# Graph kernel: residual rows of the inverse transforms on half the outputs and last in their sum, and one more turn between edges and message sums

## The chip, the cores and the metric

The kernel runs on one core of one Trainium2 chip. The metric is the device time of the whole program in microseconds (us). Before the change the median of three runs is 2021.49 us (2019.66 to 2024.59). The profiled execution took 2019.38 us, with 2017.7 us from its first to its last instruction and a mean granted TensorE clock of 0.981.

Names of engines below: PE is TensorE, DVE VectorE, ACT ScalarE, POOL GpSimd, SP the engine that queues most loads. PEld is PE's loading of weights.

## The reference, cut to what matters

There are 128 graphs of 128 nodes with 256 channels, all in float32. Layer 0, to which the change belongs, works on the normalised and rectified input `h`:

```
xc     = transpose(x)                                  # x is h here
h      = relu(bn1(conv1d(xc, conv1_w)))                # kernel width 1
h      = bn2(conv1d(h, conv2_w, pad 8))                # kernel width 17 along the nodes
x_conv = relu(h + xc)
s      = x @ w_se.T + b_se                             # three numbers per node
A      = exp(-|s_n - s_m|^2) * mask
msg    = relu(x @ w_msg.T + b_msg)
x_nmp  = A @ msg
x_in   = concat(x_conv, x_nmp)
...                                                    # a GRU cell on x_in and x gives the layer's output
```

Layer 1 is a graph convolution over the first 25 nodes of each graph, in five groups.

## The kernel before

**Front, 0 to about 537 us.** The wide convolution is done by Fourier transforms of length 80 over two windows of 64 outputs each (`OUTW`, `LW`). The spectra of the weights, the normalisation, the narrow convolution, the spectra of the nodes and the products of spectra are made here. For each graph the products are 2 x 80 = 160 rows of 256 channels, in DRAM (`yd`). The change doesn't touch this part, but it makes what the inverse transform reads.

**The loop over 32 blocks of four graphs (`BB = 4`), about 537 to 1880 us.** A block's convolution output, messages and edges are prepared in `beside_gates(i + 1)` while the gates of block i are computed in `gates(i, ...)`. The gates are four units of seven products each (a Strassen scheme, all matmuls of line 552). After each product `between()` is called, which is `step` in the main loop: that makes 28 turns in a block. A turn with an odd number advances `beside_gates` by one `yield`; an even turn, or an odd one once `beside_gates` has ended, advances layer 1, where a part of it is waiting. The fourth unit calls `nxt` at its fifth product; that runs what is left of `beside_gates` and then `gate_inputs(i + 1)`.

In `beside_gates` the steps are, in this order: messages in two halves (line 458), the inverse transform of the first 128 channels (`conv_out`, lines 441 and 443), the transposes of the edges' terms (478), the inverse transform of the other 128 channels, the edges (`edges`: one matmul at 491, an exp on ACT at 493, the product with the mask on DVE at 494), a step of `back` (the end of an earlier block; line 722 on PE and 727 on DVE), and the messages' sums in two halves (`x_nmp`, line 504). `back` also has steps beside the earlier ones. With the turns counted so, the edges come at turn 11 and the two halves of the sums at turns 15 and 17.

**The inverse transform.** The first 128 of a graph's 160 rows lie in the partitions of `ym`, one matrix per graph. The other 32 rows (`NR = 2 * LW - P`) of the four graphs are stacked in the 128 partitions of `yr`. For 128 channels, one matmul with `yr` as weights and the block-diagonal constant `idr` as moving operand fills a PSUM bank of 4 x 128 outputs with the residual rows' share; four matmuls with `ym` and the constant `idm` add the main rows' share, graph by graph:

```
nc.tensor.matmul(ps, yr[:, o * P:(o + 1) * P], idr, start=True, stop=False)
for b in range(BB):
    nc.tensor.matmul(ps[:, b * N:(b + 1) * N], ym[:, b, o * P:(o + 1) * P], idm,
                     start=False, stop=b == BB - 1)
```

DVE then scales and adds (446), and ACT rectifies into `xc` (447). All the residual rows belong to the second window, so their columns of `idr` for the first 64 outputs of each graph hold zeros.

**What sets the order.** PE's instructions follow the program's order; a scheduler lays the instructions of the other engines and the loads in order of readiness, each in a queue of its own. PSUM is a pool of eight banks that go round.

Of the kernel before, what the change touches and what calls it, by code (L numbers as in the profile page):

```python
# [8 lines left out]
F32 = mybir.dt.float32  # L9
# [4 lines left out]
P = 128  # L14
# [3 lines left out]
BB = 4  # L18
HG = 64
OUTW = 64  # L20
LW = 80
NP_ = LW // 2
WCH = 64
NR = 2 * LW - P
# [50 lines left out]
def gnn_kernel(ctx: ExitStack, tc: tile.TileContext, io, out0: bass.AP, out1: bass.AP):  # L75
    nc = tc.nc
    x, adjT = io["x"], io["adjT"]
    B, N, D = x.shape
    C = D // P
    NBLK = B // BB  # L80
    T = BB * N
# [10 lines left out]
    def bank():  # L92
        return psum.tile([P, 512], F32, tag="bank", name="bank")
# [6 lines left out]
    gt = hc.tile([P, LW], F32)  # L100
    vec = cst.tile([P, NV], F32)
    fd = hc.tile([P, 2 * LW], F32)
    idm = cst.tile([P, N], F32)
# [272 lines left out]
    wk = ctx.enter_context(tc.tile_pool(name="wk", bufs=1))  # L376
# [17 lines left out]
        loaded[i] = at, ym, yr  # L394
        hts[i] = ht

    idr = wk.tile([P, T], F32)
    nc.sync.dma_start(idr, io["idr"])

    lr = wk.tile([P, 2, BB, 32], F32)  # L400
# [33 lines left out]
    def conv_out(i):  # L434

        ht = hts[i]
        _, ym, yr = loaded[i]
        xc = wk.tile([P, C, T], F32, tag="xc", name="xc", bufs=2)
        for o in range(C):
            ps = bank()  # L440
            nc.tensor.matmul(ps, yr[:, o * P:(o + 1) * P], idr, start=True, stop=False)  # L441
            for b in range(BB):
                nc.tensor.matmul(ps[:, b * N:(b + 1) * N], ym[:, b, o * P:(o + 1) * P], idm,  # L443
                                 start=False, stop=b == BB - 1)
            u = wk.tile([P, T], F32, tag="el", name="u", bufs=2)
            nc.vector.scalar_tensor_tensor(u, ps, sc2[:, o:o + 1], ht[:, o, :], op0=ALU.mult, op1=ALU.add)
            nc.scalar.activation(xc[:, o, :], u, AF.Relu, bias=sh2[:, o:o + 1])
            yield
        xcs[i] = xc

    def messages(i):

        ht = hts[i]
        msg = wk.tile([P, BB, D], F32, tag="msg", name="msg", bufs=1)
        for b in range(BB):
            ps = bank()
            for c in range(C):
                nc.tensor.matmul(ps[:, :D + 3], ht[:, c, b * N:(b + 1) * N], wms[:, c, :], start=c == 0, stop=c == C - 1)  # L458
            nc.vector.tensor_tensor(msg[:, b, :], ps[:, :D], bms[:, :D], op=ALU.add)  # L459
            nc.vector.tensor_tensor(lr[:, 1, b, 0:3], ps[:, D:D + 3], bms[:, D:], op=ALU.add)  # L460
            if b % 2:
                nc.scalar.activation(msg[:, b - 1:b + 1, :], msg[:, b - 1:b + 1, :], AF.Relu)  # L462
                if b == 1:
                    yield
        msgs[i] = msg
        sv = lr[:, 1, :, 0:3]
        nc.vector.tensor_scalar(lr[:, 0, :, 0:3], sv, 2.0, None, op0=ALU.mult)
        s2 = wk.tile([P, BB, 3], F32, tag="sse", name="sse", bufs=2)
        nc.vector.tensor_mul(s2, sv, sv)
        nc.vector.reduce_sum(lr[:, 1, :, 3:4], s2, axis=AX.X)  # L470
        nc.vector.tensor_scalar(lr[:, 0, :, 4:5], lr[:, 1, :, 3:4], -1.0, None, op0=ALU.mult)
        yield

    def edge_terms(i):

        ps = bank()
        for k in range(2):
            nc.tensor.transpose(ps[:, k * P:(k + 1) * P], lr[:, k].rearrange("p b r -> p (b r)"), ident)
        lt = wk.tile([P, P], F32, tag="lt", name="lt", bufs=2)
        nc.scalar.copy(lt, ps[:, :P])  # L480
        rt = wk.tile([P, BB, N], F32, tag="rt", name="rt", bufs=1)
        nc.vector.tensor_tensor(rt, ps[:, None, P:2 * P].to_broadcast([P, BB, N]),
                                bm[:, :, None].to_broadcast([P, BB, N]), op=ALU.mult)
        lrs[i] = lt, rt

    def edges(i):

        at, _, _ = loaded.pop(i)
        lt, rt = lrs.pop(i)
        pd = bank()  # L490
        nc.tensor.matmul(pd, lt, rt.rearrange("p b n -> p (b n)"), start=True, stop=True)
        e = wk.tile([P, BB, N], F32, tag="e", name="e", bufs=1)
        nc.scalar.activation(e.rearrange("p b n -> p (b n)"), pd, AF.Exp)
        nc.vector.tensor_mul(e, e, at)  # L494
        A_s[i] = e

    def x_nmp(i):

        e, msg = A_s.pop(i), msgs.pop(i)
        xn = wk.tile([P, C, T], F32, tag="xn", name="xn", bufs=2)  # L500
        for c in range(C):
            ps = bank()
            for b in range(BB):
                nc.tensor.matmul(ps[:, b * N:(b + 1) * N], msg[:, b, c * P:(c + 1) * P], e[:, b, :],  # L504
                                 start=True, stop=True)
            if c:
                nc.vector.tensor_copy(xn[:, c, :], ps)
            else:
                nc.scalar.copy(xn[:, c, :], ps)
            yield  # L510
        xns[i] = xn
# [162 lines left out]
    def back_loads(i):  # L674

        ae = l1.tile([P, GW], F32, tag="ae", name="ae", bufs=1)
        nc.sync.dma_start(ae[:n4], io["adjE"][i])
        dc = l1.tile([P, GW], F32, tag="dce", name="dce", bufs=1)
        nc.sync.dma_start(dc, dvf.rearrange("t p -> (t p)")[i * GW:(i + 1) * GW].partition_broadcast(P))
        return ae, dc  # L680
# [207 lines left out]
    def beside_gates(i):  # L888

        ends = back(i - 2, *back_loads(i - 2)) if i > 1 else iter(())  # L890
        if i < NBLK:
            parts = messages(i)
            next(parts)
            yield
            next(parts)
            next(ends, None)
            yield
            inverse = conv_out(i)
            next(inverse)
            next(ends, None)  # L900
            yield
            edge_terms(i)
            next(ends, None)
            yield
            for _ in inverse:
                yield
            edges(i)
            yield
            next(ends, None)
            yield  # L910
            yield from x_nmp(i)
        for _ in ends:
            yield
            if i == NBLK:
                yield
# [4 lines left out]
    for _ in beside_gates(0):  # L920
        pass
# [46 lines left out]
def _spectral_constants():  # L968

    import numpy as np  # L970

    f = np.arange(1, NP_)

    def rows(t):

        t = np.asarray(t)
        c = np.cos(2 * np.pi * np.outer(np.arange(NP_ + 1), t) / LW)
        s = np.sin(2 * np.pi * np.outer(np.arange(NP_ + 1), t) / LW)
        return c, s

    gt = np.zeros((P, NP_, 2))
    fd = np.zeros((P, 2, NP_, 2))
    inv = np.zeros((2, NP_, 2, P))
    c, s = rows(np.arange(KW))
    for r in range(4):
        k = slice(32 * r, 32 * r + KW)
        gt[k, 0, 0], gt[k, 0, 1] = c[0], c[NP_]
        gt[k, 1:, 0], gt[k, 1:, 1] = c[f].T, s[f].T
    for w in range(2):
        n0, n1 = max(0, w * OUTW - PAD), min(P, w * OUTW + OUTW + PAD)  # L990
        c, s = rows(np.arange(n0, n1) - (w * OUTW - PAD))
        fd[n0:n1, w, 0, 0], fd[n0:n1, w, 0, 1] = c[0], c[NP_]
        fd[n0:n1, w, 1:, 0], fd[n0:n1, w, 1:, 1] = c[f].T, (-s[f] - c[f]).T
        c, s = rows(np.arange(OUTW))
        n = slice(w * OUTW, (w + 1) * OUTW)
        inv[w, 0, 0, n], inv[w, 0, 1, n] = c[0] / LW, c[NP_] / LW
        inv[w, 1:, 0, n], inv[w, 1:, 1, n] = 2 * c[f] / LW, -2 * s[f] / LW
    inv = inv.reshape(2 * LW, P)
    idr = np.zeros((BB, NR, BB, P))
    for b in range(BB):  # L1000
        idr[b, :, b] = inv[P:]
    d = {"gt": gt.reshape(P, LW), "fd": fd.reshape(P, 2 * LW), "idm": inv[:P], "idr": idr.reshape(P, BB * P)}
    return {k: np.ascontiguousarray(v, dtype=np.float32) for k, v in d.items()}


def _lay_out(a):
# [18 lines left out]
    d["w2t"][:, :KW] = w2  # L1025
    d["w2t"] = d["w2t"].reshape(P, 2, -1, WCH // 4, P)
    d.update(_spectral_constants())
    d["wms"] = cc(np.concatenate([w["w_msg"], w["w_se"]]).T)
    d["bms"] = cc(np.concatenate([w["b_msg"], w["b_se"]]))
# [60 lines left out]
```

## Time and profile before

| stretch, us | length | PE busy | DVE busy | ACT busy | POOL busy | granted clock |
|---|---|---|---|---|---|---|
| 0 to 537, front | 537 | 495.78 | 311.89 | 158.47 | 152.26 | 0.94 |
| 537 to 1880, loop | 1343 | 1320.56 | 937.62 | 494.40 | 431.22 | 1.00 |
| 1880 to 2018, end | 138 | 132.41 | 65.34 | 52.43 | 17.19 | 1.00 |

Busy times are unions: two overlapping instructions of one engine count once. A float32 matmul of the program is two records in the trace, so counts of PE are twice those in the code. A record's duration holds its latency as well, which overlaps the next record; how fast PE streams is seen from the distance of starts, or in the chain of waits, whose pieces abut. In the loop a block without layer 1 takes 38.9 us, from one matmul on `e` to the next block's.

### The profile page before, as it was taken

The page shows a single profiled execution, that of the slowest core. Times are in us where ns is not written, and L with a number is a line of the kernel's source. Part 1 is how long each engine was busy: PE and PEld are TensorE (multiplying, and loading weights), DVE is VectorE, ACT ScalarE, POOL GpSimd, SP SyncE. Part 2 cuts the span into 40 slices and gives each one's busy share as a digit, 9 for nine tenths or more (in the row PEclk, how much of TensorE's full clock was granted, in tenths as well). Part 3 has the DMA queues.
Part 4 walks back from the last instruction along what each step waited for, and adds up shares of the span by engine and source line. Part 5 has one row for each costly group of instructions (what it writes and reads, how often), then busy time and mean ns, then how long its engine had stood idle before and what let it go on. Part 6 is the DMA issues. An engine that isn't in the chain of part 4 may idle for free.

```text
span 2017.7 us, 29868 instructions
## 1 busy us (share of the span) xinstructions
PE 1948.7 (97%) x10418; PEld 1665.4 (83%) x10418; DVE 1314.8 (65%) x3287; ACT 705.3 (35%) x1406; POOL 600.7 (30%) x681
## 2 busy tenths in 40 slices
PE   8899998999899999999999999999999999999998
PEld 7888877988678888888878888888878888888887
DVE  6667445845477676777755676777755677777643
ACT  3334113421133333333334434333334433333344
POOL 3111441125233343343321143343322143343300
PEclk8899999999899999999999999999999999999999
DMA  9883885459843223223323523223322523321225
GB/s 353 329 284 117 283 280 183 157 170 308 247 134 88 66 74 98 71 68 89 105 68 83 154 69 99 76 69 78 113 71 81 155 70 91 83 69 41 61 81 154
DMA packets 248421, 265.89 MB, mean 132 GB/s; under 512 B 106802, under 2 KB 223751, under 8 KB 243663
## 3 DMA queue, kind: packets, MB, share of 16 engines
q1 hardware_dynamic: 239935, 225.71, 38.2%
q10 hardware_dynamic: 8336, 38.28, 4.9%
q8 instruction: 83, 1.36, 0.3%
q14 instruction: 67, 0.55, 0.1%
HBM read 178.79 MB, written 85.14 MB: 131 GB/s over the span
## 4 chain that ended last, share of the span: by engine, by line
PE 84%; DVE 6%; DMA 5%; issue 2%; POOL 2%; ACT 1%; SPq 0%; DVEq 0%; POOLq 0%; ACTq 0%
PE bank L552 39%; PE bank L307 6%; PE bank L458 6%; PE bank L871 5%; PE bank L223 5%; PE bank L811 5%; PE bank L504 3%; PE bank L238 3%; PE bank L302 3%; PE bank L443 3%; PE bank L441 3%; DMA ln<-in_x_dram 2%; PE bank L790 1%; PE bank L209 1%; DVE e L494 1%
## 5 line engine op out<-in xcount | busy, mean ns | idle before, releaser
L552 PE MATMUL bank<-t,sw 128*128 128x256 f32 x1152 | 291.1, 380 | 0.0
L565 POOL TENSOR_TENSOR u<-u,m 128x256 f32<-128x256 f32 x128 | 92.9, 726 | 654.6 <-ACT m L563 590.2
L552 PEld LDWEIGHTS bank<-t,sw 128*128 128x128 f32 x1152 | 213.4, 190 | 29.6 <-issue 2.8
L552 PE MATMUL bank<-t,wih 128*128 128x256 f32 x768 | 197.3, 379 | 0.0
L552 PEld LDWEIGHTS bank<-t,wih 128*128 128x128 f32 x768 | 143.2, 190 | 18.9 <-issue 0.5
L299 POOL TENSOR_TENSOR vs<-v 128x512 f32<-128x512 f32 x78 | 102.2, 1330 | 139.5 <-DMA v<-vd 53.8
L223 PE MATMUL bank<-wc,ht 128*128 128x256 f32 x512 | 127.2, 404 | 13.1 <-ACT ht L210 11.9
L458 PE MATMUL bank<-wms,ht 128*128 128x259 f32 x512 | 125.3, 388 | 5.2 <-DMA ht<-htd 5.2
L223 PEld LDWEIGHTS bank<-wc,ht 128*128 128x128 f32 x512 | 102.4, 205 | 30.4 <-ACT ht L210 15.0
L458 PEld LDWEIGHTS bank<-wms,ht 128*128 128x128 f32 x512 | 99.3, 194 | 21.0 <-issue 5.6
L552 PE MATMUL bank<-xc,wih 128*128 128x256 f32 x384 | 114.7, 380 | 0.0
L552 PE MATMUL bank<-xn,wih 128*128 128x256 f32 x384 | 114.5, 380 | 0.0
L552 PE MATMUL bank<-t,whh 128*128 128x256 f32 x384 | 114.4, 379 | 0.0
L871 PE MATMUL bank<-w,hh 128*125 128x256 f32 (+9 forms) x480 | 113.5, 380 | 0.5 <-DVE hh L816 0.5
L552 PE MATMUL bank<-ht,whh 128*128 128x256 f32 x384 | 110.4, 381 | 0.0
L297 DVE SCALAR_TENSOR_TENSOR s<-X 128x256 f32<-128x256 f32 x78 | 47.8, 615 | 90.7 <-PE bank L307 90.3
L811 PE MATMUL bank<-ax,w 128*128 128x500 f32 (+8 forms) x416 | 106.9, 396 | 0.0
L462 ACT ACTIVATE msg<-msg 128x512 f32<-128x512 f32 x64 | 40.3, 630 | 173.8 <-DVE msg L459 161.0
L157 POOL TENSOR_TENSOR rs<-ve,mhalf 128x4 f32<-128x4 f32 x32 | 32.3, 1010 | 227.0 <-DVE ve L155 227.0
L871 PEld LDWEIGHTS bank<-w,hh 128*125 128x125 f32 (+9 forms) x480 | 84.3, 178 | 18.7 <-issue 0.9
L443 PEld LDWEIGHTS bank<-idm,ym 128*128 128x128 f32 x512 | 68.1, 194 | 30.9 <-issue 30.9
L504 PEld LDWEIGHTS bank<-e,msg 128*128 128x128 f32 x512 | 65.2, 192 | 33.3 <-DVE e L494 31.5
(190 smaller groups left out, 4291.6 us busy)
## 6 DMA issues: line engine op xcount, KB each, us to landing
v<-vd SPq DMA_DIRECT2D x80, 512.0 KB
vd<-sp SPq DMA_DIRECT2D x8, 2560.0 KB
yd<-ys ACTq DMA_DIRECT2D x40, 512.0 KB
w<-in_w_dram SPq DMA_DIRECT2D x40, 512.0 KB
htd<-ht ACTq DMA_DIRECT2D x32, 512.0 KB
ht<-htd SPq DMA_DIRECT2D x32, 512.0 KB
ym<-yd SPq DMA_DIRECT2D x32, 512.0 KB
xt<-in_xT_dram SPq DMA_DIRECT2D x32, 512.0 KB
```

Source lines behind the costliest of these rows:

```text
L223: nc.tensor.matmul(pv[:, bb, :], ht[:, c, b * N:(b + 1) * N], wc1[:, c, :], start=c == 0, stop=c == C - 1)
L238: nc.tensor.matmul(ps[:, bb * 2 * LW:(bb + 1) * 2 * LW], h1[:, 2 * h + bb, c * P:(c + 1) * P], fd, start=True, stop=True)
L299: nc.gpsimd.tensor_tensor(vs, vr, vi, op=ALU.add)
L302: nc.tensor.matmul(p1[:, :D], a[:, c], vs[:, c], start=c == 0, stop=c == C - 1)
L307: nc.tensor.matmul(ps[:, k * D:(k + 1) * D], u[:, c], w[:, c], start=c == 0, stop=c == C - 1)
L443: nc.tensor.matmul(ps[:, b * N:(b + 1) * N], ym[:, b, o * P:(o + 1) * P], idm, start=False, stop=b == BB - 1)
L458: nc.tensor.matmul(ps[:, :D + 3], ht[:, c, b * N:(b + 1) * N], wms[:, c, :], start=c == 0, stop=c == C - 1)
L504: nc.tensor.matmul(ps[:, b * N:(b + 1) * N], msg[:, b, c * P:(c + 1) * P], e[:, b, :], start=True, stop=True)
L552: nc.tensor.matmul(ps, w, d, start=n == 0, stop=n == len(pairs) - 1)
L565: nc.gpsimd.tensor_tensor(got["u4"], got["u2"], got["m5"], op=ALU.add)
L811: nc.tensor.matmul(pv[:, q - q0, :], w1s[k5 + g][:, c, q * P:(q + 1) * P], xv[:, c], start=c == 0, stop=c == C - 1)
L871: nc.tensor.matmul(ps[:n1, :D], hh[:, q, at:at + n1], w2s[k5 + g][:, q, :], start=q == 0, stop=q == HID // P - 1)
```

## The change

It has three parts.

1. The residual matmul writes only the second 64 outputs of each graph. `idr` shrinks from 4 x 128 to 4 x 64 columns, and the output becomes four runs of 64 in the bank, 128 apart. Its purpose is to leave out the columns whose constant is zero.
2. It becomes the last of the five matmuls instead of the first[...]. The start flag goes to the first main matmul.
3. One more `yield` stands between the edges and the messages' sums, so that the edges have one more odd turn (two turns of the gates) before PE comes to need them.

```
-    idr = wk.tile([P, T], F32)
+    idr = wk.tile([P, BB, N - OUTW], F32)
...
             ps = bank()
-            nc.tensor.matmul(ps, yr[:, o * P:(o + 1) * P], idr, start=True, stop=False)
             for b in range(BB):
                 nc.tensor.matmul(ps[:, b * N:(b + 1) * N], ym[:, b, o * P:(o + 1) * P], idm,
-                                 start=False, stop=b == BB - 1)
+                                 start=b == 0, stop=False)
+
+            nc.tensor.matmul(ps.rearrange("p (b n) -> p b n", b=BB)[:, :, OUTW:], yr[:, o * P:(o + 1) * P], idr,
+                             start=False, stop=True)
...
             next(ends, None)
             yield
+            yield
             yield from x_nmp(i)
...
-    idr = np.zeros((BB, NR, BB, P))
+    idr = np.zeros((BB, NR, BB, P - OUTW))
     for b in range(BB):
-        idr[b, :, b] = inv[P:]
+        idr[b, :, b] = inv[P:, OUTW:]
```

More of the change, by code (lines that the diff above doesn't have):

```diff
@@ L998, in _spectral_constants @@
     inv = inv.reshape(2 * LW, P)
-    idr = np.zeros((BB, NR, BB, P))
+    idr = np.zeros((BB, NR, BB, P - OUTW))
     for b in range(BB):
-        idr[b, :, b] = inv[P:]
-    d = {"gt": gt.reshape(P, LW), "fd": fd.reshape(P, 2 * LW), "idm": inv[:P], "idr": idr.reshape(P, BB * P)}
+        idr[b, :, b] = inv[P:, OUTW:]
+    d = {"gt": gt.reshape(P, LW), "fd": fd.reshape(P, 2 * LW), "idm": inv[:P], "idr": idr.reshape(P, BB, P - OUTW)}
     return {k: np.ascontiguousarray(v, dtype=np.float32) for k, v in d.items()}
```

## The prediction, made before the changed kernel ran

> **What bounds the kernel now.** I read four things in order: the page's busy shares, the stretch of the gate loop alone, the waits of TensorE inside it, and the chain of waits over one block.
>
> The first line is the page's busy shares, the second is the answer for the stretch from 537 to 1880 us, which holds the loop over the 32 blocks of four graphs (columns: stretch, length, then busy us and count of PE, PEld, DVE, ACT, POOL, then granted clock and DMA share).
>
> ```profile
> PE 1948.7 (97%) x10418; PEld 1665.4 (83%) x10418; DVE 1314.8 (65%) x3287; ACT 705.3 (35%) x1406; POOL 600.7 (30%) x681
> 537.00:1880.00 1343.00, 1320.56 (x6471) 1118.88 (x6472) 937.62 (x2237) 494.40 (x883) 431.22 (x519) 1.00 0.33 90
> ```
>
> PE is busy 98% of this stretch at clock 1.00, DVE 70%, the others under 40%. The change touches only this stretch. The waits of PE there, complete (us in total, times, longest):
>
> ```profile
> PE bank L504 <- DVE e L494: 19.8, 28, 2.2
> PE bank L661 <- issue: 2.0, 1, 2.0
> PE bank L441 <- DVE lr L471: 1.3, 1, 1.3
> ```
>
> So PE waits once per block for one thing, the edges `e`, and for nothing else. The groups give the prices (count, then busy us and mean ns of one); every f32 matmul leaves two records, so L441's 128 records are 32 blocks x 2 channel halves x 2:
>
> ```profile
> L552 PE MATMUL bank<-t,sw 128*128 128x256 f32 x1152 | 291.1, 380 | 0.0
> L443 PE MATMUL bank<-idm,ym 128*128 128x128 f32 x512 | 68.3, 277 | 0.0
> L441 PE MATMUL bank<-idr,yr 128*128 128x512 f32 x128 | 65.9, 597 | 1.3 <-DVE lr L471 1.3
> ```
>
> The mean of one record holds its latency, which overlaps the next record. What a matmul costs the queue is read from the chain, whose pieces abut (start, us, what):
>
> ```profile
> 1328.59 0.86 PE bank L441 x2
> 1329.45 0.89 PE bank L443 x8
> 1330.34 2.59 PE bank L552 x12
> ...
> 1340.55 0.64 DVE e L494
> 1341.19 0.04 issue
> 1341.23 1.16 PE bank L504 x8
> 1342.39 1.73 PE bank L552 x8
> 1344.12 0.89 PE bank L504 x8
> ```
>
> A 512-column record takes 0.43 us of PE, a 256-column one 2.59/12 = 0.216, a 128-column one 0.111. The whole block is such pieces end to end, broken only where `e` enters the chain.
>
> **What the Trainium skill says.** "TensorE: Matmul & The Clock Gate", section "Back-to-back issue gap", gives N/2.4 + 2.5 ns per warm matmul. Counting each f32 column twice per record, that is 429, 216 and 109 ns for 512, 256 and 128 columns, which is what the chain shows; the page's sustained 131 ns for 512 columns is not what this f32 stream does. "PSUM — Partial Sum Buffer", section "The four PSUM rules", says that the first matmul clears the written-bits of the whole bank and that a later one overwrites where a bit is clear and adds where it is set. So the new order (four main matmuls, the start flag on the first alone, then the residual one) needs no further instruction; the trace of before cannot show that. "ScalarE: Activation LUTs", section "What ACT_TABLE_LOAD costs", has 1283 ns for the load, and the record ahead of the exp shows 1.28 us. No page that I read prices a matmul whose output has steps, as the new one has.
>
> **The residual matmul.** Per block and channel half, two records of 512 columns become two of 256 (4 graphs x the second 64 outputs). The price of a 256-column record is that of L552, contiguous in its output: 0.216. Saved: 64 x (0.86 - 2 x 0.216) = 27.4 us, all on the PE stream, because PE has no slack beside it. The upper bound of the new record is 0.43 (the stepped output costs as much as the full row), which would save 0. I take 0.216: the same number of columns stream and the same number of elements land. The loaded constant idr falls from 256 KB to 128 KB, once, behind other loads: 0.
>
> **Residual last instead of first.** PE order only. Weight loads (190 ns records) stay hidden: the load of the first main matmul now lies under an L552 record instead of a residual one, and the load of `yr` under the last main one. L443 has the same kind of neighbours in its own row of eight and runs at 0.111 each. The main operand ym is now needed first and yr last. In the changed build's queue for loads ym stands ahead of all four yr loads, where it stood between them; in the loop neither was waited for. 0.
>
> **The extra turn.** The edges are queued at turn 11 of 28, the messages' sums at turns 15 and 17. With the extra turn the sums go to 17 and 19; the built order shows the eight L504 records moved so, and the DVE order still has ab, then e, where they were. What they wait for, as the timelines of PE, DVE and ACT show it (start, us, engine, line):
>
> ```profile
> 1378.91 0.59 PE L552 MATMUL bank<-xn,wih 128*128 128x256 f32 x2
> 1380.14 1.16 PE L504 MATMUL bank<-e,msg 128*128 128x128 f32 x8 [0.64 <-DVE e L494]
> 1381.14 0.60 PE L552 MATMUL bank<-xc,wih 128*128 128x256 f32 x2
> ```
> ```profile
> 1374.94 0.75 DVE L446 SCALAR_TENSOR_TENSOR u<-bank,bn,ht 128x512 f32<-128x512 f32 x1 [0.65 <-PE bank L443]
> ...
> 1378.87 0.59 DVE L727 TENSOR_TENSOR ab<-bank,dce 128x424 f32<-128x424 f32 x1
> 1379.38 0.71 DVE L494 TENSOR_TENSOR e<-e,at 128x512 f32<-128x512 f32 x1
> ```
> ```profile
> 1376.72 1.28 ACT L493 ACT_TABLE_LOAD   x1
> 1378.01 0.60 ACT L493 ACTIVATE e<-bank 128x512 f32<-128x512 f32 x1
> ```
>
> The two L552 records from 1378.91 stream until 1379.34; the next starts at 1380.14: 0.80 us lost. The first eight L504 then take 1.00 us to the next start, where the later eight take 0.89: 0.11 more. So 0.91 us per wait. Of the 28, the longest is in block 0's preparation, where no gate turns lie between and the turn moves nothing; 27 x 0.91 = 24.6 us.
>
> Is the turn enough? Turns 15 and 16 (now ahead of the sums) stream 2 x 4 x 0.216 = 1.73 us, in place of 0.80 needed, so 0.9 us remain. The residual's saving does not eat this: the chain to `e` starts at the end of the second inverse transform (DVE u at 1374.94), which itself moves up. From there `e` needs 5.2 us and PE arrives after 4.6 + 1.73 = 6.3.
>
> What queues behind: `xn` comes about 1.7 us of PE stream later. Its user, the t of DVE, begins at 1355.31 for the block whose second L504 ends at 1345.0; the copy lies between. Some 8 us of slack are left. The wait moves from PE to nobody. Layer 1 runs on even turns and on odd ones after the side work has ended, so it gets one step fewer in a block; from 1040 to 1184 us, where it runs, PE has no wait at all, so its work is only spread: 0. Its last part runs after the loop on unchanged code: 0.
>
> **Sum.** 27.4 + 24.6 = 52.0; 2021.5 - 52.0 = 1969.5 us.
>
> **Rivals.**
> A, the wait takes another form: DVE, POOL or the eight banks of PSUM bind once PE runs a block in 38.9 - 0.86 - 0.91 = 37.1 us. Against it: DVE is busy 28.5 us in such a block, ACT and POOL 14 each. For it: DVE is dense around `e`, with hardly any idle from 1377.5 to 1382.8, and PE gets there sooner. If half of the wait's worth comes back: 1982; if all: 1994.
> B, the stepped output streams at the old price: only 24.6 us come, 1997. Nothing in the trace of before shows such an output, for or against.
> C, slower: each run of 64 outputs breaks the stream and pays the 0.11 us that a restart cost above. Eight runs per residual matmul are 0.9 us, 64 of them 56 us, against the 52 gained: 2026. Against it: PE writes other partial-bank outputs (259 columns, 212 columns) at their streaming price.
>
> **Chances.** Both gains in full 0.80 (1969); A 0.11 (1982 to 1994); B 0.06 (1997); C 0.03 (2026). The forecast is the first case. Three runs of before spread by 5 us, so that case alone covers 1963 to 1975; the range goes to 1982 to take in half of A. Faster 0.96, within 0.3% 0.01, slower 0.03.
>
> **What would show it.** Right: PE's wait for `e` gone from the loop but for the one in the preparation; two records of the residual in 0.43 us of the chain; a steady block of 37.1 us instead of 38.9; PE busy for 99% or more of the loop; no new PE wait over 2 us. Wrong at the residual: its pair still at 0.86, or longer. Wrong at the turn: L504 still waiting, or another PE line with a wait of some 0.5 us in each block. Wrong in the side effects: a DMA or a bank in PE's waits where layer 1 starts, near 1000 and 1450 us.

## The result

The changed kernel takes 1966.7 us (median of four runs, 1964.24 to 1968.31) against 2022.14 us before (2019.66 to 2024.59). The ratio is 0.9725, with a 95% interval of 0.9708 to 0.9742. The forecast was 1969.5 us. A second measurement on another chip gave 0.9733 (0.9716 to 0.975).

The profiled spans differ by 52.8 us (2017.7 and 1964.9 us). Of the changed kernel, the first line below is the page's busy shares; the second is its loop (stretch, length, busy us and count of each engine, granted clock, DMA share), which now ends some 52 us sooner:

```profile
PE 1910.8 (97%) x10418; PEld 1664.1 (85%) x10418; DVE 1301.2 (66%) x3287; ACT 702.1 (36%) x1406; POOL 610.3 (31%) x681
537.00:1828.00 1291.00, 1285.47 (x6476) 1120.35 (x6475) 925.78 (x2243) 492.50 (x884) 441.74 (x519) 1.00 0.35 94
```

The share of the span is the same 97% as before: PE lost work and idle time together. In the loop PE is busy 1285.47 of 1291 us, 99.6% against 98.3%. DVE has the same work in less time, 72%.

Line numbers are two higher from the inverse transform on (552 is 554, 494 is 496, 504 is 506), and three higher from 911 on. In the inverse transform the main matmuls are now L442 and the residual one L445. PE's waits in the loop, complete:

```profile
PE bank L663 <- issue: 3.4, 1, 3.4
PE bank L506 <- DVE e L496: 2.1, 1, 2.1
```

Twenty-seven of the 28 waits for `e` are gone; the one left is the preparation of block 0. The new residual's group and the chain over one block:

```profile
L445 PE MATMUL bank<-idr,yr 128*128 128x256 f32 x128 | 38.5, 383 | 0.0
```
```profile
1271.68 0.89 PE bank L506 x8
...
1301.18 0.89 PE bank L442 x8
1302.07 0.43 PE bank L445 x2
1302.51 0.86 PE bank L554 x4
...
1305.81 3.02 PE bank L554 x14
1308.83 0.89 PE bank L506 x8
```

The reader is to see three things. The residual pair costs 0.43 us where it cost 0.86, and the main eight cost 0.89 as before. The first eight L506 records of a block cost 0.89 like the second eight, where they had cost 1.16 with the wait ahead of them. And no engine but PE is named in the block any more. From the start of one block's sums to the next's it is 1308.83 - 1271.68 = 37.15 us. Before it was 1341.23 - 1302.32 = 38.91; the sums at 1341.23 stand in the prediction, those one block earlier are

```profile
1302.32 1.16 PE bank L504 x8
```

### The profile page after: what moved, and what is told of

It reads as the page before. It is cut to its first block, busy times and chain, and to the rows that moved or that the text cites. A ratio compares the mean times of both kernels' runs of the same rounds, so it can differ in the third digit from the quotient of the medians.

```text
span 1964.9 us, 29914 instructions
## 1 busy us (share of the span) xinstructions
PE 1910.8 (97%) x10418; PEld 1664.1 (85%) x10418; DVE 1301.2 (66%) x3287; ACT 702.1 (36%) x1406; POOL 610.3 (31%) x681
## 4 chain that ended last, share of the span: by engine, by line
PE 91%; DMA 4%; DVE 3%; POOL 1%; issue 0%; ACT 0%; SPq 0%; POOLq 0%; DVEq 0%; ACTq 0%
PE bank L554 44%; PE bank L307 6%; PE bank L460 6%; PE bank L873 5%; PE bank L223 5%; PE bank L813 5%; PE bank L238 3%; PE bank L442 3%; PE bank L302 3%; PE bank L506 3%; DMA ln<-in_x_dram 2%; PE bank L445 1%; DMA v<-vd 1%; PE bank L493 1%; PE bank L792 1%; PE bank L724 1%
## 5 line engine op out<-in xcount | busy, mean ns | idle before, releaser
L572 DVE TENSOR_TENSOR u<-bank,u 128x256 f32<-128x256 f32 x128 | 53.7, 420 | 73.3 <-PE bank L554 73.2
L594 ACT ACTIVATE nn<-nn,vec 128x512 f32<-128x512 f32 x64 | 46.2, 722 | 131.1 <-DVE nn L593 131.1
```

## The experiments

My theory: the two parts are separate gains on a PE stream that has no slack. The residual's gain is its columns; the turn's gain is distance between `e` and its first user. The rivals: one part carries all of it, or each needs the other; the place in the sum matters; the wait only moves to DVE, a bank or another line.

### The residual part alone

```
@@ beside_gates @@
             next(ends, None)
             yield
-            yield
             yield from x_nmp(i)
```

> The change without the extra turn: the residual matmul on the second 64 outputs, last in the sum. Theory (two separate gains on a saturated PE stream): 27.4 us off, about 1994.5 us, a ratio of 0.986; PE still waits for e 28 times for about 20 us, because the chain to e starts at the end of the second inverse transform and moves up with it. Rival (the residual's gain is eaten by the wait, or the turn was needed to cash it): PE's wait for e grows by 0.4 us a block and only some 15 us come, 2007 us. Rival (all of it is the residual): 1967 us.

Measured: 1990.54 us, ratio 0.986 (0.984 to 0.988). Of PE's waits in the loop, the first line:

```profile
PE bank L506 <- DVE e L496: 20.2, 28, 2.0
```

The wait is as it was (19.8 us in 28 before). It grew by nothing to speak of: from the start of DVE's `u`, the first step after the second inverse transform, to the first user of `e` it is 5.21 us (1314.74 to 1319.95), and before it was 5.20 (1374.94 to 1380.14). So the chain to `e` moved up by as much as PE's stream did. A block takes 38.07 us (sums from 1319.95 to 1358.02), 0.84 less than before. Both rivals fall. The narrow residual matmul as the first of the five was not run, so whether the first part of the change needs the second is not shown.

### The extra turn alone, and with the residual last on all columns

The first is the kernel before with one `yield` more. The second adds the new place in the sum at the old width:

```
-            nc.tensor.matmul(ps, yr[:, o * P:(o + 1) * P], idr, start=True, stop=False)
             for b in range(BB):
                 nc.tensor.matmul(ps[:, b * N:(b + 1) * N], ym[:, b, o * P:(o + 1) * P], idm,
-                                 start=False, stop=b == BB - 1)
+                                 start=b == 0, stop=False)
+            nc.tensor.matmul(ps, yr[:, o * P:(o + 1) * P], idr, start=False, stop=True)
```

> The extra turn alone, the residual matmul as before (512 columns, first). Theory: 27 waits of 0.91 us go, 24.6 us off, about 1997.5 us, a ratio of 0.988; no PE wait in the loop but the one in the preparation; a steady block of 38.0 us. Rival (the wait only moves): PE waits elsewhere for DVE or a bank, 2010 to 2022 us.

> The extra turn, and the residual matmul last in the sum but still on all 512 columns. Theory (the place in the sum costs and brings nothing): the same as the extra turn alone, about 1997.5 us, within 4 us. Rival (the place in the sum matters, by the load of its weights under a short matmul or by yr being needed later): a difference of more than 5 us, either way, and the five matmuls' piece of the chain no longer 1.75 us.

Measured: 1999.44 us, ratio 0.9898 (0.9881 to 0.9916), and 1994.94 us, ratio 0.988 (0.9864 to 0.9896). The intervals overlap. The medians lie 4.5 us apart, half a microsecond more than I had allowed, but the profiled spans lie 2.2 us apart the other way (1993.3 and 1995.5), so nothing is told by it. The blocks settle it: the chain of each, first the turn alone, then with the residual last,

```profile
1319.86 0.86 PE bank L441 x2
1320.72 0.89 PE bank L443 x8
...
1327.94 0.89 PE bank L504 x8
```
```profile
1321.66 0.89 PE bank L442 x8
1322.55 0.86 PE bank L444 x2
...
1329.74 0.89 PE bank L504 x8
```

has the same 1.75 us for five matmuls in either order. A block takes 38.01 us (to the next sums at 1365.95) and 38.00 us (to 1367.74). So the turn is worth 0.90 us a block, and the place in the sum nothing. The rival of the first falls too: with the turn alone PE's list for the loop has three lines, each of one wait (2.2, 2.0 and 1.8 us), and none comes back block by block.

The parts add up by the block: 0.84 for the residual and 0.90 for the turn make 1.74, and both together give 38.91 - 37.15 = 1.76. The whole times are coarser: by the medians on this chip the residual brought 28.4 us and the turn 19.5, or 24.0 with the residual last, against 53.7 to 55.4 for the whole change on other chips.

One cheaper remedy was not tried. In the timelines of before, the exp of `e` ends at 1378.01 + 0.60 = 1378.61, but DVE starts the product only at 1379.38, since `ab` (from 1378.87) stands ahead of it in DVE's queue. With the two exchanged, `e` would come up to 0.51 us sooner by my estimate (1379.38 - 1378.87), and part of the 0.91 would go without a turn.

### How much of the turn is surplus

In the changed kernel's DVE timeline the product that makes `e` ends at 1306.98 + 0.71 = 1307.69, and PE's timeline starts its first user at 1308.67, as PE gets there:

```profile
1306.98 0.71 DVE L496 TENSOR_TENSOR e<-e,at 128x512 f32<-128x512 f32 x1
1308.67 1.05 PE L506 MATMUL bank<-e,msg 128*128 128x128 f32 x8
```

0.98 us are over. To measure that, the product is done more than once (the mask holds 0 and 1):

```
-        nc.vector.tensor_mul(e, e, at)
+        for _ in range(2):          # 3 in the second kernel
+            nc.vector.tensor_mul(e, e, at)
```

> The changed kernel with DVE's product of e and the mask done twice (the mask holds 0 and 1, so the result stays). The second product and the nh addition that the queue puts between them make e 0.64 + 0.33 = 0.97 us later. In the changed kernel's trace e ends at 1307.69 and its first user starts at 1308.67, so 0.98 us are free. Theory (the turn's worth is distance in PE's stream, and the surplus is free): no loss or hardly any, 1967 to 1970 us, PE's waits for e at most 0.1 us a block. Rival (the stream of DVE is the near bound, so added DVE work costs in any place): 27 x 0.6 to 1 us, 1983 to 1993 us.

> The same product three times. With what the queue puts between them (nh 0.33, o 0.67) e comes 2 x 0.64 + 0.33 + 0.67 = 2.3 us later than in the changed kernel. Theory: 0.98 of it is free, 1.3 us plus 0.11 for the restart is lost in each of the 26 blocks without layer 1, some 37 us, 2004 us; PE waits for e again in 26 to 28 blocks. Rival (no limit met): 1967 us.

Measured: 1974.92 us and 2009.62 us, where a kernel with the changed kernel's time (the next experiment's) gave 1966.74 us on the same chip. From 600 to 1850 us, PE's list of waits is empty in the first and has one line in the second. Below it is the chain's piece for the first eight sums of a block in the first kernel (lines are one higher here, so L507 is the sums):

```profile
PE bank L507 <- DVE e L497: 30.1, 25, 1.2
```
```profile
1312.87 1.07 PE bank L507 x8
```

The second loses 43 us; I had worked out 37. It is the wait come back: over the whole loop the waits for `e` are 36.1 us in place of 2.1, and 27 times the first eight sums take 1.13 us in the chain in place of 0.89, which makes 40.5.

The first was to be free or nearly so and cost 8 us, so my theory missed its size. In its timelines the second product ends at 1312.66, only 0.04 us before PE would get to the sums (the four records from 1311.84 stream until 1312.70); PE starts them at 1312.81, and the first eight take 1.07 us in the chain. That is 0.18 us more than in the changed kernel, in each of 26 blocks, or 4.7 us. Another 2.1 us are waits at the start of the loop (4.2 in place of 2.1), where block 0's preparation has no turns to hide it. So a product that only just comes in time is not free. If the 0.18 is taken off, some 0.8 of the 0.98 us are free; that is an estimate, as no smaller delay was run. The rival, that DVE's stream is the near bound, would have cost at least 0.6 us a block in the first; it falls.

### More turns

```
             yield
             yield
+            yield
+            yield
+            yield
             yield from x_nmp(i)
```

> The changed kernel with two more turns between edges and sums than it has (three added in all); the sums stand at turns 21 and 23 of 28, against 17 and 19. Theory: nothing more to gain, as PE no longer waits there; nothing to lose while xn comes before its t on DVE at turn 26: 1967 us within 4. Rival (xn too late for t, so that the next block's third product waits, or DVE's work piles up at the end of the block): 5 to 40 us slower with a PE wait on DVE's t.

The expectation counts one turn too few: the kernel that ran has three more turns than the changed kernel, four added in all, and its sums stand at turns 23 and 25.

Measured: 1966.74 us, ratio 0.9729 (0.9714 to 0.9743), the changed kernel's time. The sums can stand four turns of the side work later than before the change, three later than in the changed kernel, with nothing gained and nothing lost over the latter. From 600 to 1850 us PE waits for nothing, so `xn` still comes in time for its t.

### The same distance by moving the edges instead

```
+            edges(i)
             for _ in inverse:
                 yield
-            edges(i)
             yield
             next(ends, None)
             yield
-            yield
             yield from x_nmp(i)
```

> The changed kernel with its extra turn taken out between edges and sums, and the edges queued one odd turn earlier instead, ahead of the second inverse transform; the turn left over stands after that transform, so the sums stay at turns 17 and 19 as in the changed kernel. Edges and sums are then two odd turns further apart than before the change instead of one. Theory: PE had no wait left to lose, so the time is that of the changed kernel, 1967 us within 4. Rival (the place of the exp and its table load on ACT, ahead of the second inverse transform's work, costs a wait on DVE or ACT): 5 to 20 us slower, with a new PE wait.

The expectation has the turns wrong here as well. The extra turn is gone, so the sums are back at turns 15 and 17, and with the edges at turn 9 the distance is three odd turns, just as in the changed kernel (11 to 17), not one more.

Measured: 1982.79 us, ratio 0.9829 (0.9806 to 0.9851). By the medians that is 16 us slower than the changed kernel on another chip, by the ratios about 1%. My theory had expected no difference and missed; the rival was right that a wait appears, though not where it put it. From 600 to 1850 us PE's list has one line, and the chain shows what is in front of it:

```profile
PE bank L493 <- DVE rt L484: 7.1, 26, 0.9
```
```profile
1310.03 0.43 DVE st L714
1310.46 0.60 DVE rt L484
1311.06 0.04 issue
1311.11 1.12 PE bank L493 x2
```

The edges' matmul needs `rt`, which DVE makes from the transposes one odd turn before. That distance was two odd turns (7 to 11) and had been enough; pulled up to one, it costs some 0.5 us a block, which takes 1311.11 - 1273.44 = 37.67 us against 37.15. I had counted the distance behind the edges and not the one ahead of them. No wait for `e` is left from 600 us on, so moving the edges does cure that one; it opens another. A turn placed behind `e` lengthens the short distance and shortens none.

### The price of a stepped output

```
-            nc.tensor.matmul(ps.rearrange("p (b n) -> p b n", b=BB)[:, :, OUTW:], yr[:, o * P:(o + 1) * P], idr,
+            nc.tensor.matmul(ps.rearrange("p (b n) -> p b n", b=BB)[:, :, 0:N:2], yr[:, o * P:(o + 1) * P], idr,
                              start=False, stop=True)
```

> The changed kernel, but the residual matmul's 256 outputs go to every second column of the bank instead of the second 64 of each graph; the sum is therefore another one (the residual rows' share lands on other outputs). Theory (PE streams by the count of columns, whatever the steps of its output): the pair still 0.43 us in the chain, the time that of the changed kernel. Rival (a stepped output has a price that runs of 64 hide): the pair at 0.5 us or more.

One execution took 1967.77 us, and in its chain

```profile
1296.54 0.89 PE bank L442 x8
1297.43 0.43 PE bank L445 x2
1297.86 1.29 PE bank L554 x6
```

the pair stands at 0.43. Runs of 64, steps of two columns and the contiguous outputs of the gates all stream at the same price.

### A version that is faster still

With PE at 99.6% of the loop what is left to gain in the loop is less PE work. The edges' matmul is 512 columns in which each group of 32 rows is non-zero in a quarter:

```
-        pd = bank()
-        nc.tensor.matmul(pd, lt, rt.rearrange("p b n -> p (b n)"), start=True, stop=True)
+        pd = [bank() for _ in range(BB)]
+        for b in range(BB):
+            nc.tensor.matmul(pd[b][:, :N], lt[32 * b:32 * b + 32, :], rt[32 * b:32 * b + 32, :], start=True, stop=True)
...
-        nc.scalar.activation(e.rearrange("p b n -> p (b n)"), pd, AF.Exp)
+        for b in range(BB):
+            nc.scalar.activation(e[:, b, :], pd[b][:, :N], AF.Exp)
```

`rt` becomes a copy of 128 columns without the mask.

> A try at more, on the changed kernel: the edges' matmul (512 columns on a block-diagonal operand) is split into four, one for each graph, on its own 32 rows of PE and in a bank of its own, 128 columns each; DVE copies 128 columns instead of masking 512, and ACT does four exps of 128 columns instead of one of 512. Theory (PE's stream is the bound, and four row groups stream side by side): the 0.86 us piece falls to between 0.2 and 0.45 us, 13 to 21 us off, 1946 to 1954 us, if e is not late again: the four exps take some 0.4 us more on ACT, PE comes 0.4 to 0.65 earlier, and 0.98 us was free, so a wait of 0 to 0.2 us may come back (up to 8 us with its restart). Rival (four banks at once and the later e cost PE more than the streaming saves): 1967 to 1990 us.

Measured: 1961.72 us, ratio 0.9703 (0.9689 to 0.9717); 5 us faster than the 1966.74 us of the kernel with more turns on the same chip, and less than the 13 us expected at least. Beside the changed kernel on one chip:

> The changed kernel once more, beside the split edges on one chip, to tell their difference apart. Expected from its first measurement: a ratio of 0.9725 to before, within 0.0015.

> The changed kernel with the edges' matmul in four row groups, measured again beside the changed kernel. Its steady block was 36.92 us (from one first sum's start to the next, 1306.91 to 1343.83) against 37.15, so 0.23 us in 32 blocks, 7 us or a ratio of 0.969 to before. Rival (no real difference): 0.9725.

Measured: the changed kernel takes 1968.66 us, 0.9733 (0.9716 to 0.975), and the split one 1960.44 us, 0.9695 (0.968 to 0.971). The intervals are apart: 8 us faster than the changed kernel. The chain of the split kernel at the edges shows why it is not more (L555 is the gates, L493 the edges):

```profile
1300.81 0.86 PE bank L555 x4
1301.67 0.43 PE bank L493 x8
1302.11 1.06 PE bank L555 x4
1303.17 0.72 PE bank L725 x4
```

The eight small records take 0.43 us in place of 0.86, as expected, but the four records after them take 1.06 where four take 0.86. The net is 0.23 us a block (36.92 against 37.15), 7 us in 32 blocks. PE's list of waits has no line of the edges. The starts in PE's timeline divide the 0.20 us: a pair of L555 records next to another starts 0.43 us before it, but the pair ahead of the small records starts 0.52 us before them (1301.08 and 1301.60), and the first pair behind them takes 0.53 to the next start (1302.04 and 1302.57). So about half is paid on the way into the small tiles and half on the way back. Weights, else loaded ahead of their matmul, begin to load on both sides only as it starts (1301.60 and 1302.04). "TensorEngine Tiling (Array Packing)", one of the pages of the Trainium skill, says in its section "Key Properties" that a change of tiling mode drains the engine, which would fit; that the drain is the cause of the 0.20 us was not tried by itself.

## Why the prediction was right

**The bound.** The step "PE has no slack beside it" carried all the rest, and held: every removal showed in the block nearly one for one, 0.84, 0.90 and 1.76 us against 0.86, 0.91 and 1.77. PE's wait "once per block" was 28 waits for 32 blocks, which the sum of 27 took into account.

**The residual matmul.** 0.86 to 2 x 0.216 was taken from L552's row, and the pair is at 0.43. Forecast 27.4 us; 0.84 x 32 blocks = 27 us, and 28.4 us by the medians of that experiment (2018.95 to 1990.54). The upper bound (0.86, rival B) and the broken stream (rival C) are both excluded by that pair, and finer steps cost no more.

**Last instead of first.** Costed at nothing; 38.00 and 38.01 us a block.

**The extra turn.** 0.91 us a wait was forecast and 0.90 a block measured; 27 waits went and the one in block 0's preparation stayed, as forecast. By the whole time the turn alone brought 19.5 us (interval of the ratio: 17 to 24), a little less than the 24.6 forecast, and 24.0 with the residual last. The surplus was worked out in two ways that do not agree: "0.9 us remain", and 6.3 against 5.2 us, which leaves 1.1. The 4.6 us in the second is a slip. From the start of `u` to PE's arrival the lines give 1379.34 - 1374.94 = 4.40, and 4.40 + 1.73 is 0.98 over the 5.15 that `e` needs. The changed kernel's timelines show just this 0.98.

**Rival A,** in which the wait takes another form, did not come. DVE works 27.79 us in a block of 37.15 and kept up. Nor did the places named for side effects show anything: no PE wait begins at 1000 or 1450 us.

**What was off.** The sum, 52.0 us, meets the profiled spans' 52.8; the medians' 55.4 and the second measurement's 53.7 spread by no more than the runs do. PE's wait at L663 (the transposes of the degrees) is 3.4 us instead of 2.0, once, in the first block. It is 4.4 in the second measurement of the same kernel and 2.0 to 6.5 in the experiments, so it tells nothing of the change.

## What to carry to other kernels

Where one engine streams without a gap in a stage, and its list of waits there has a single line, the price of a change can be read off in pieces of the chain: count the columns that go and the idle that ends, and add them. To remove a wait of an engine that works in program order, put other work of that engine between producer and consumer, and check the distance in front of the producer as well: moving the producer up can break that one. Columns whose constant is zero are work like any other; steps in the output cost nothing here, so the useful columns can be picked out.

## What was not expected of the hardware

Splitting a 512-column matmul into four row groups halved its own piece (0.86 to 0.43 us), but going into the small tiles and back cost 0.20 us, about half on each side. A product that ended 0.04 us before PE would have come to its user still cost 0.18 us a time, though no wait of that length is listed.
